# Layer 2's 512x512 product by seven block products, with its sums on GpSimd, and VectorE's set-up work moved

## The chip, the cores and the metric

One core of one Trainium2 chip runs the whole program. The metric is the device time of one execution in microseconds (us). All numbers are float32. The engines are called TensorE (PE; PEld is its weight load), VectorE (DVE), ScalarE (ACT), GpSimd (POOL) and SyncE (SP, which issues most DMAs).

## The reference, cut to what matters

Four residual layers act on x of 8 sequences of 128 tokens and width 512, 1024 tokens in all. Each layer has a first part (its conditioning) and a feed-forward part.

- Layer 0: a gated product with small per-sequence adapters, `silu(gate) * up` with 1376 hidden columns, a product back to 512, then a routed feed-forward.
- Layer 1: two chains of small adapters.
- Layer 2: attention with 32 query and 8 key heads of 128, over 512 cached positions (fetched through a block table) and the 128 new ones, then the feed-forward that this change is about.
- Layer 3: a routed product, then a second one with 64 small experts.

Layer 2's feed-forward, on the attention's output y:

```python
H = einsum('btd,od->bto', y, W) + b                     # the 512x512 product
z = einsum('btd,dr->btr', y, A)                         # rank 32
anchors = arange(1, T, 2)                               # every second token
H_slice = H[:, anchors, :8]
delta_slice = einsum('bar,er->bae', z[:, anchors], LiMEs)
H_scale = maximum(max(abs(H_slice)), EPS)               # one number over all tokens
d_scale = maximum(max(abs(delta_slice)), EPS)
probs = softmax(0.5 * H_slice / H_scale + 0.5 * delta_slice / d_scale)
...                                                     # weights: soft top 2 of 8, normalised
p_mix = einsum('bte,er->btr', repeat(weights, 2), LiMEs)
return H + einsum('btr,ro->bto', z * p_mix, Bmat) * 0.5
```

The result is added to x.

## The kernel before, in words

Activations lie feature by token: x is [128, 4, 1024], four chunks of 128 features. A product of 512 by 512 is done in blocks of 128, each f32 matmul of the program leaving two records in the trace.

**Two ways of multiplying.** The plain way uses eight products of half-size blocks. In most places the kernel uses seven instead (the scheme with sums s1 to s4 of the left blocks and t1 to t4 of the right ones, and three to four additions behind the products). `gates_by_seven` does so for layer 0's gates in stages f = 1 to 10, about 13.4 us each; the class `Seven` for layer 3. Its `begin` does the first product and copies it out, its `go_on` the others; the additions of its partial results (`u`, `p1`) are on VectorE, from PSUM banks `even` and `odd`. Layer 2's W was multiplied in the plain way by `product(b)`: one block of 128 tokens, 16 matmuls of 128 columns, eight times. The tile of its result is called h.

**Stages.** Loads and layer 0's gates of stage 0 (0 to 26 us; matmuls gu, rank sums tgm and tum); stages 1 to 10 of the gates (to 162; matmuls g, additions `up` and p); down product, layers 0 and 1 (to 297); attention in 32 steps (to about 1347); layer 2's feed-forward (to 1392); layer 3 (to the end).

**Attention's beginning.** Step n needs rows of the cache: `gather(n, "k")` and `gather(n, "v")` issue eight indirect DMAs each on GpSimd's queue. k's rows (tiles kn) are turned by a DMA (kt) ahead of the scores, v's rows (vals) are wanted by the step's last product, av. `run` orders them by hand: before the loop `gather(1, "v")` (L1326), in step 0 `gather(2, "k")` (L1379). The q products q_one, q_five, q_six are the seven-product scheme again.

**Layer 2's feed-forward.** At the end of the attention, `product(0)` already runs while the last step waits for R, the inverse sums that a DMA spreads over the partitions; then oT (av times R), its sums os, the out products wo_one to wo_six and their additions y. In `layer2`, `turn` transposes y into y2T for two last blocks of tokens, `low` gives z, `anchors` hd. `routing` reduces hd to big, GpSimd's partition_all_reduce gives top, and some twenty short instructions on VectorE and ScalarE (lg, p, m) give the weights. `gains` transposes them (pT), multiplies (pmix) and gives zp = z times p_mix. `delta(g)` adds zp by Bm to h with contraction 32, for half g of the tokens, and adds h to x. Between these, TensorE is filled with `product` and with the preparation of layer 3 (`weights_turned`: W3p, wB3p, copied by ScalarE to W; `fold_scores`: qwp, qbp, fkp, gkp). Layer 3 begins with midp, and then fp, the first `Seven`, whose left sums W3s are made by GpSimd (L2004), as are Bws. `anyone` is another partition_all_reduce on GpSimd, a check of the attention's sums, read at the end.

**Order.** Each engine runs its instructions in a fixed order. Where the code says `kept(...)`, an instruction stays behind the one traced before it on its engine; this sets the order of issue and is no wait. All else is placed by the framework's scheduler, by its own estimate of when inputs are ready; so the order on GpSimd and of the unpinned matmuls is not the order of the source. Matmuls of one PSUM bank and the VectorE instructions that read it wait for each other.

Of the kernel before, what the change touches and what calls it, by code (L numbers as in the profile page):

```python
# [47 lines left out]
def forward(ctx: ExitStack, tc: tile.TileContext, a: dict, out: bass.AP):  # L48
# [35 lines left out]
    for c in range(DC):  # L84
        sp.dma_start(x[:, c, 0:512], a["xT"][c * P : (c + 1) * P, 0:512])
        if c == 0:
            first = gate_weights(0, act, (slice(0, 1), slice(1, DC)))
            sp.dma_start(ids0_i, a["lora_ids"].partition_broadcast(P))
# [41 lines left out]
    def ints(name, n, where=const):  # L130
        ti = where.tile([P, n], I32, tag=name + "_i", name=name + "_i")
        sp.dma_start(ti, a[name].partition_broadcast(P))
        tf = where.tile([P, n], F32, tag=name, name=name)
        dve.tensor_copy(tf, ti)
        return tf

    def rows(name, n, where=const):
# [34 lines left out]
    mask1 = const.tile([P, NB], F32, tag="mask1", name="mask1")  # L172
    dve.tensor_scalar(mask1, ids1, p_div16, None, ALU.is_equal)

    kvrow = {}
    for what, order in (("v", "p (b c j) -> p b c j"), ("k", "p (b j c) -> p b c j")):
        selp = w0.tile([P, NB, 4, 4], F32, tag="selp", name="selp_" + what)
        dve.tensor_tensor(  # L180
            selp,
            table.rearrange(order, b=NB, c=4),
            block32.unsqueeze(1).unsqueeze(1).to_broadcast([P, NB, 4, 4]),
            ALU.mult,
        )
        page = const.tile([P, NB * 4], F32, tag="page", name="page_" + what)
        dve.tensor_reduce(page.rearrange("p (b c) -> p b c", c=4), selp, AX.X, ALU.add)
        dve.tensor_scalar(page, page, 32.0, p_mod32, ALU.mult, ALU.add)
        kvrow[what] = const.tile([P, NQ, NB * 4], I32, tag="kvrow_" + what, name="kvrow_" + what)
        for qd in range(NQ):  # L190
            dve.tensor_scalar(kvrow[what][:, qd, :], page, float(NQ), float(qd), ALU.mult, ALU.add)


    bias3 = const.tile([P, NB, 8], F32, tag="bias3", name="bias3")
    dve.tensor_tensor(
        bias3,
        eight.unsqueeze(1).to_broadcast([P, NB, 8]),
        lang.unsqueeze(2).to_broadcast([P, NB, 8]),
        ALU.is_equal,
    )  # L200
    dve.tensor_scalar(bias3, bias3, 5.0, None, ALU.mult)

# [115 lines left out]
    with c0:  # L318
# [75 lines left out]
        def gates(f, ws, between):  # L394

            fw = min(P, FF - f * P)
            banks = [bank(f"gu_{f}_{j}") for j in range(4)]
            for js in ((0, 1), (2, 3)):
                for c in range(DC):
                    if js[0] and c == 2:  # L400
                        between()
                    for k, w in enumerate(ws):
                        for j in js:
                            mmq(banks[j][:fw, k, :], w[:, c, :fw], x[:, c, quarter(j)], k == 0 and c == 0, False)
            return banks
# [25 lines left out]

        def gates_by_seven(f, A):

# [12 lines left out]
            for g in range(TG):  # L446
# [12 lines left out]
                kept(dve.tensor_tensor(p1, six[:, 0], p1, ALU.add))  # L459
                B.append((one, two, six, p1, u, b21, b22, t4))  # L460
            for one, two, six, _, _, b21, b22, t4 in B:
                into(one[:, 0], a12, b21, False)
                into(two[:, 1], s4, b22, False)
                into(six[:, 0], a22, t4, False)
# [74 lines left out]
        lora_gates(0, banks)  # L539
        rot, angles, turn_angles = rotary(tc, rp, w0, lens, part, rows, kept)  # L540
        for f in range(1, NF):
            after = f + 1 < NF and weight_sums(f + 1, gate_weights(f + 1))
            gates_by_seven(f, A)
            A = after
            if f == 2:
                down_loaded()
            for i in itertools.islice(angles, 3 * (f > 1)):
                kept(i)
            if f == NF // 2:
                AW = [down_weights(0, wop.tile([P, 3, NH, P], F32, tag="os", name="wds_0"))]  # L550
# [242 lines left out]
def attention(tc, a, x, ident, lens, kvrow, part, ww, wop, ypool, sums, rot, eps, psa, c2, chunks, mm):  # L793
# [524 lines left out]
    def run(pool_, end_of, bank, keep):  # L1318
# [6 lines left out]
        roots(1)  # L1325
        gather(1, "v")  # L1326
        rotated(1)
# [7 lines left out]
        for n, (qd, p) in enumerate(steps):  # L1335
# [41 lines left out]
            if n == 0:  # L1377
                next(sums_of)
                gather(2, "k")  # L1379
            every(sums_of)  # L1380
# [37 lines left out]
        every(outputs(n))  # L1418
        end.product(0, "st", bank)
        leave(n)  # L1420
# [312 lines left out]
def ending(  # L1733
# [57 lines left out]
    def load_w2():  # L1791
        W["2"] = tile_of_w2([P, DC, D], "WT2")
        kept(sp.dma_start(W["2"], chunks(a["W2T"])))
# [13 lines left out]
    def low(g, bank):  # L1807

        ps = bank("mm", [P, P], f"z2_{g}")
        for c in range(DC):  # L1810
            for j in range(HB):
                b = g * HB + j
                mmq(ps[slot(j), :], A2[:, c, :], Y2T[0][:, c, b * P : (b + 1) * P], c == 0, c == DC - 1)
        dve.tensor_copy(zq[:, g, :], ps)
# [10 lines left out]

    H = {}

    def shifted():

        for c in range(DC):  # L1830
            kept(act.activation(x[:, c, :], x[:, c, :], AF.Identity, bias=bcol[:, c : c + 1]))

    def product(b, tag, bank):

        ps = bank(tag, [P, DC, P], f"h_{b}")
        for o in range(DC):
            for c in range(DC):
                mmq(
                    ps[:, o, :], W["2"][:, c, o * P : (o + 1) * P], Y2T[0][:, c, b * P : (b + 1) * P],
                    o == 0 and c == 0, False,  # L1840
                )
        H[b] = ps

# [52 lines left out]
    def gains(bank):  # L1896
# [8 lines left out]
        for g in range(TG):  # L1905
            for j in range(HB):
                b = g * HB + j
                mmq(pm[slot(j), g, :], Li, pT[:, b * 64 : (b + 1) * 64], g == 0, True)
        zp = L3.w3.tile([P, TG, P], F32, tag="zp", name="zp")
        dve.scalar_tensor_tensor(  # L1910
            zp.rearrange("p g (t two) -> p g t two", two=2),
            zq.rearrange("p g (t two) -> p g t two", two=2),
# [3 lines left out]
            ALU.mult,  # L1916
        )
        Z["zp"] = zp

    def delta(g):  # L1920

        zp, Bm = Z["zp"], L3.Bm
        for o in range(DC):
            for j in range(HB):
                mmq(H[g * HB + j][:, o, :], Bm[slot(j), o * P : (o + 1) * P], zp[slot(j), g, :], False, True)
        for j in range(HB):
            b = g * HB + j
            t = x[:, :, b * P : (b + 1) * P]
            dve.tensor_tensor(t, H[b], t, ALU.add)

    def open3(w3, ex_sm):
# [21 lines left out]
        L3.steps = experts("l3", L3.wmr, "logits", 2.0, bias3, None, None, x, None, width=WR)  # L1955
        L3.zgT = w3.tile([P, DC, NT], F32, tag="zgT", name="zgT")

    def copied(shape, name, ps, dst=None):
# [18 lines left out]
    def fold_scores(bank):  # L1977
        ps = bank("mm", [P, D], "qwp")
        for o in range(DC):
            mmq(ps[slot(o), :], L3.wq[:, o, :], L3.W[:, o, :], True, True)  # L1980
        qw = copied([P, D], "qw3", ps)
        ps = bank("mm", [P, P], "qbp")
        for o in range(DC):
            mmq(ps[slot(o), :], L3.wq[:, o, :], L3.wBT[:, o, :], True, True)
        qb = copied([P, P], "qb3", ps)
# [20 lines left out]

    def right_sums(b11, b12, b21, b22, t):
        t1, t2, t3, t4 = (t[:, k] for k in range(4))
        for o, l, r in ((t1, b12, b11), (t2, b22, t1), (t3, b22, b12), (t4, b21, t2)):
            dve.tensor_tensor(o, l, r, ALU.subtract)  # L2010
        return b11, b21, b22, t1, t2, t3, t4
# [9 lines left out]
    class Seven:  # L2021
# [19 lines left out]
        def go_on(self):  # L2041
# [11 lines left out]
            self.into(even[:, 1], a22, t4)  # L2053

    S = {}

# [8 lines left out]
    def fold_ranks(bank):  # L2065
        L3.F = L3.w3.tile([P, DC, D], F32, tag="F3", name="F3")
        tw = room("o7", [P, 2, 4, 2, P], "W3s")
# [118 lines left out]

    def layer2(y2, bank, held=lambda: None, do=range(NB)):

        for b in do:
            turn(y2, b, bank)  # L2190
        for g in range(TG):
            if g or len(do) > HB:
                low(g, bank)
                anchors(g, bank)

        where = ["mm"]

        def free(tag, shape, name):
            return bank(where[0], shape, name)

        turning, folding = weights_turned(free), fold_scores(free)
        for b in range(HB):
            if b not in H:
                product(b, "av" if b == HB - 1 else "st", bank)
                next(turning, None)
        routing()
        gains(bank)
        product(HB, "av", bank)
        next(turning, None)
        delta(0)  # L2210
        where[0] = "st"
        for b in range(HB + 1, NB):
            product(b, "mm", bank)
            for _ in turning:
                pass
            next(folding, None)
        delta(1)

    def layer3(bank, between=lambda: None):
# [38 lines left out]
        prepare=prepare, load_w2=load_w2, load_aw=load_aw, turn=turn, low=low, anchors=anchors,  # L2258
        product=product, shifted=shifted, open3=open3, layer2=layer2, layer3=layer3,
    )  # L2260
# [65 lines left out]
```

## Time and profile before

| what | us |
|---|---|
| median of 3 runs (lowest, highest) | 1496.21 (1494.47, 1498.43) |
| profiled execution | 1493.37 |
| its span, first to last instruction | 1491.6 |
| TensorE busy (share of the span) | 1476.2 (99%) |
| VectorE, GpSimd, ScalarE busy | 1069.6, 855.0, 561.9 |
| windows of layer 2, 1343 to 1393: TensorE, VectorE, GpSimd busy | 49.4, 21.3, 10.4 of 50 |
| granted clock of TensorE | 1.00 |

A group line of the profile reads: line of the code, engine, operation, output<-input, shapes, count, then busy time and mean of one, and the idle time of its engine just ahead of it with what ended that. L followed by a number is a line of the kernel. A window line has the window, its length, then for PE, PEld, DVE, ACT and POOL the busy time with the number of instructions, the clock, the share of DMA and the GB/s. "Lost" time of TensorE, used below, is how much later a matmul started than the rate of its neighbours would have it; idle time, which the views print, is somewhat shorter, since a matmul's record runs past the start of the next.

### The profile page before, as it was taken

How to read it: one execution, taken by the hardware profiler on the slowest of the kernel's cores; microseconds unless marked ns; L12 is line 12 of the kernel's file. 1: busy time of each engine (PE TensorE's matmuls, PEld its weight loads, DVE VectorE, ACT ScalarE, POOL GpSimd, SP SyncE). 2: the span in 40 equal slices, each digit the busy share in tenths (PEclk: the TensorE clock that was granted, in tenths of full speed). 3: DMA queues.
4: the chain of work that ended last, by engine and by line, in shares of the span. 5: the costliest groups of instructions: out<-in, count | busy, mean ns of one | idle time of the engine just before them, and what ended most of it. 6: DMA issues, size and time to landing. Idle time of an engine off the chain costs nothing.

```text
span 1491.6 us, 18090 instructions
## 1 busy us (share of the span) xinstructions
PE 1476.2 (99%) x5603; PEld 937.3 (63%) x5603; DVE 1069.6 (72%) x2121; ACT 561.9 (38%) x1422; POOL 855.0 (57%) x876
## 2 busy tenths in 40 slices
PE   9999999999999999999999999999999999999998
PEld 7888787455555555555565555555555555559886
DVE  4665524388888787877778778777877878855475
ACT  1111101044444554444455445455445455431110
POOL 2242104567776777777677777677777767632310
PEclk9999999999999999999999999999999999999999
DMA  7411001213546444554444456445445534333001
GB/s 241 118 44 32 1 1 55 94 35 102 175 135 204 134 127 130 155 174 133 140 149 120 124 155 182 125 135 152 131 130 160 174 109 135 111 116 98 1 9 52
DMA packets 155082, 171.44 MB, mean 115 GB/s; under 512 B 52577, under 2 KB 125473, under 8 KB 154849
## 3 DMA queue, kind: packets, MB, share of 16 engines
q1 hardware_dynamic: 136832, 133.18, 30.4%
q0 software_dynamic: 17056, 36.49, 7.6%
q8 instruction: 47, 0.77, 0.2%
q10 hardware_dynamic: 1088, 0.52, 0.1%
q14 instruction: 59, 0.48, 0.1%
HBM read 129.36 MB, written 40.76 MB: 114 GB/s over the span
## 4 chain that ended last, share of the span: by engine, by line
PE 91%; DVE 3%; issue 2%; DMA 2%; ACT 0%; POOL 0%; SPq 0%; ACTq 0%; DVEq 0%; POOLq 0%
PE st L1165 18%; PE av L1217 17%; PE g L362 8%; PE q_six L971 8%; PE q_five L971 6%; PE q_one L971 5%; PE wo_two L971 5%; PE dn L362 5%; PE wo_six L971 4%; PE wo_one L971 4%; PE h L1753 2%; PE z L1753 2%; PE eo_l L53 2%; PE o L1753 1%; PE midp_l L53 1%
## 5 line engine op out<-in xcount | busy, mean ns | idle before, releaser
L914 POOL DMA_INDIRECT kn<-in_k_cache,kvrow_k x256 | 270.0, 1055 | 77.3 <-issue 71.8
L914 POOL DMA_INDIRECT vals<-in_v_cache,kvrow_v x256 | 271.6, 1061 | 73.5 <-issue 61.7
L1217 PE MATMUL av<-pT,vals 128*128 128x512 f32 x640 | 290.7, 592 | 0.2 <-DVE oT L1227 0.2
L1169 ACT ACTIVATE pT<-st,hide 128x512 f32<-128x512 f32 x256 | 175.9, 687 | 191.2 <-PE st L1165 167.9
L1165 PE MATMUL st<-qT,kT 128*128 128x512 f32 x512 | 236.0, 593 | 0.5 <-DMA qT<-turned_new 0.5
L1217 PEld LDWEIGHTS av<-pT,vals 128*128 128x128 f32 x640 | 121.4, 190 | 152.7 <-issue 149.5
L1070 POOL TENSOR_TENSOR vq<-q,txq 128x256 f32<-128x256 f32 x128 | 121.2, 976 | 135.7 <-ACT sqq L1044 95.5
L1165 PEld LDWEIGHTS st<-qT,kT 128*128 128x128 f32 x512 | 96.5, 190 | 109.5 <-issue 102.3
L1185 DVE TENSOR_TENSOR part<-pT 128x512 f32<-128x512 f32 x128 | 88.4, 691 | 76.6 <-ACT pT L1169 63.2
L971 PE MATMUL q_one<-q,x 128*128 128x384 f32 x256 | 93.0, 486 | 0.0
L1044 ACT ACTIVATE sqq<-q 128x128 f32<-128x128 f32 x252 | 78.2, 310 | 11.3 <-DVE q L1020 4.7
L971 PEld LDWEIGHTS q_one<-q,x 128*128 128x128 f32 x256 | 48.5, 190 | 39.8 <-issue 14.1
L971 PE MATMUL q_six<-q_s,xs_all 128*128 128x384 f32 x192 | 69.8, 486 | 0.0
L1025 ACT COPY q<-q_one 128x256 f32<-128x256 f32 x32 | 11.9, 372 | 152.1 <-PE q_one L971 133.5
L971 PE MATMUL wo_one<-o,oT 128*128 128x256 f32 x256 | 65.8, 379 | 0.3 <-DVE oT L1227 0.3
L1165 PE MATMUL st<-qT,kTn 128*128 128x512 f32 x128 | 65.4, 592 | 0.0
L971 PE MATMUL wo_two<-o_s,os 128*128 128x256 f32 x256 | 60.6, 380 | 0.3 <-DVE os L930 0.3
L1169 ACT ACTIVATE pT<-st,rs 128x512 f32<-128x512 f32 x64 | 44.0, 687 | 38.5 <-PE av L1217 16.5
L971 PEld LDWEIGHTS wo_one<-o,oT 128*128 128x128 f32 x256 | 48.6, 190 | 13.9 <-DVE oT L1227 0.5
L429 POOL TENSOR_TENSOR ws<-wu 128x256 f32<-128x256 f32 (+1 forms) x9 | 6.4, 712 | 88.4 <-DMA wu<-in_WuT 81.9
L1201 ACT COPY rows<-rows 32x32 f32<-32x32 f32 x96 | 20.7, 216 | 92.8 <-DVE rows L1196 85.9
L362 PE MATMUL g<-xs,ws 128*128 128x256 f32 (+1 forms) x240 | 55.1, 379 | 0.0
(461 smaller groups left out, 2843.5 us busy)
## 6 DMA issues: line engine op xcount, KB each, us to landing
turned_new<-qkt SPq DMA_DIRECT2D x120, 160.0 KB
turned_cached<-kt SPq DMA_DIRECT2D x128, 128.0 KB
kT<-turned_cached SPq DMA_DIRECT2D x32, 512.0 KB
R<-sums SPq DMA_DIRECT2D x32, 512.0 KB
qT<-turned_new SPq DMA_DIRECT2D x30, 512.0 KB
q<-in_WqT SPq DMA_DIRECT2D x8, 1024.0 KB
o<-in_WoT SPq DMA_DIRECT2D x8, 1024.0 KB
kn<-in_k_cache,kvrow_k POOLq DMA_INDIRECT x256
```

Source lines behind the costliest of these rows:

```text
L53: pe.matmul(o, lhsT, rhs, start=start, stop=stop)
L362: pe.matmul(o, lhsT, rhs, start=start, stop=stop, skip_group_check=True)
L914: kept(pool.indirect_dma_start(out=d[:, c, :], out_offset=None, in_=kc if what == "k" else vc, in_offset=bass.IndirectOffsetOnAxis(ap=kvro ...
L971: kept(pe.matmul(o, l[:, c, :], r[:, c, :], start=start and c == 0, stop=c == 1, skip_group_check=True))
L1044: kept(act.activation(sq, S[n][m][:, j, i, :], AF.Square, accum_out=S[n]["ssq"][:, j, col : col + 1]))
L1070: kept(pool.tensor_tensor(to, t[:, b, :, hi : hi + 64], wx[:, b, lo : lo + 64].unsqueeze(2).to_broadcast(list(to.shape)), ALU.mult,))
L1165: kept(pe.matmul(ps, s["kT"][:, c, 4 * j : 4 * j + 4, :] if c < 4 else s["kn"][:, j], s["qT"][:, :, REP * j : REP * (j + 1), :].rearrange( ...
L1169: kept(act.activation(pT[:, c, :, :].rearrange("p i t -> p (i t)"), ps, AF.Exp, **(dict(bias=hide[:, b, c : c + 1]) if c < 4 else dict(bia ...
L1185: kept(dve.tensor_tensor(o, l, r, ALU.add))
L1201: kept(act.copy(rows[0:32, g, :], rows[32 * g : 32 * g + 32, 0, :]))
L1217: kept(pe.matmul(ps, v[:, c, :], pT[:, c, :, :].rearrange("p i t -> p (i t)"), start=c == 0, stop=c == NC - 1, skip_group_check=True,))
L1753: return pe.matmul(o, lhsT, rhs, start=start, stop=stop, skip_group_check=True)
```

## The change

1. **Layer 2's product.** `product` is gone. `Second`, a subclass of `Seven`, does W times y2T in four parts (token half g, output half k), seven products each of 128x128 weights and 256 columns. Its opening (`second_begun`: products a11 b11, with the copy of it on ScalarE, and a12 b21) of the parts (0,0) and (0,1) takes the place of `product(0)` in the attention's last step. The sums of W and of both halves of y2T are made by GpSimd. Two of the four partial results go into x by separate additions of `u` and `p1`; the other half by `delta`, which adds now from four half banks per k.
2. **zp twice.** `gains` has zp a second time with neighbouring groups of 32 partitions exchanged, by four copies on ScalarE, since a bank of `Second` holds two blocks of tokens side by side.
3. **Order in layer 2.** `go_on` of (0,0) in front of `low` and `anchors`, (0,1) in front of `routing`; (1,0) is opened behind `routing` and continued behind `gains`; (1,1) behind `delta(0)`. `low` for g = 1, `delta`, qwp and qbp are pinned.
4. **VectorE's set-up.** The integer casts and the tables of the block table and of layer 3's bias (29 instructions) move from the start into stages f = 1 and 2 of the gates, ahead of `up`; the 23 angle instructions, three a stage, from behind a stage (f = 2 on) to ahead of `up` in it (f = 3 on).
5. **First loads.** The first chunk of x comes in two DMAs, the first gate weights in three pairs in place of two; the load of lora_ids goes behind x's second chunk; stage 0's first matmuls take the token halves one after the other.
6. **First gathers.** `gather(1, "v")` and `gather(2, "k")` exchange places.

The diff, cut to its core:

```diff
-            first = gate_weights(0, act, (slice(0, 1), slice(1, DC)))
+            first = gate_weights(0, act, (slice(0, 1), slice(1, 2), slice(2, DC)))
...
-        dve.tensor_copy(tf, ti)
+        to_float.append((tf, ti))
...
+    def tables():
+        for tf, ti in to_float:
+            yield dve.tensor_copy(tf, ti)
+        yield dve.tensor_scalar(mask1, ids1, p_div16, None, ALU.is_equal)
...
             B.append((one, two, six, p1, u, b21, b22, t4))
+            for i in meanwhile:
+                kept(i)
...
-            gates_by_seven(f, A)
+            gates_by_seven(f, A, itertools.islice(tabled, 15) if f < 3 else itertools.islice(angles, 3))
...
-            for i in itertools.islice(angles, 3 * (f > 1)):
-                kept(i)
...
-        gather(1, "v")
+        gather(2, "k")
...
-                gather(2, "k")
+                gather(1, "v")
...
-        end.product(0, "st", bank)
+        for k in range(2):
+            end.second_begun(0, k, bank("st", [P, 2, 256], f"h_0_{k}_even"))
...
-    def product(b, tag, bank):
-        ps = bank(tag, [P, DC, P], f"h_{b}")
-        for o in range(DC):
-            for c in range(DC):
-                mmq(
-                    ps[:, o, :], W["2"][:, c, o * P : (o + 1) * P], Y2T[0][:, c, b * P : (b + 1) * P],
...
+        for b in range(HB):
+            act.copy(zp[slot(b), 1], zp[slot(b ^ 1), 0])
...
-        for o in range(DC):
-            for j in range(HB):
-                mmq(H[g * HB + j][:, o, :], Bm[slot(j), o * P : (o + 1) * P], zp[slot(j), g, :], False, True)
-        for j in range(HB):
-            b = g * HB + j
-            t = x[:, :, b * P : (b + 1) * P]
-            dve.tensor_tensor(t, H[b], t, ALU.add)
+        for other in range(2):
+            for i in range(2):
+                for b in range(HB):
+                    k, h = b % 2, (b + other) % 2
+                    ps, o = H[g][k].c[i, b // 2][0], 2 * k + i
+                    kept(mmq(ps[:, h * P : (h + 1) * P], Bm[slot(b), o * P : (o + 1) * P], zp[slot(b), other, g, :], False, True))
+        for k, f in enumerate(H[g]):
+            for (i, j), (ps, _) in f.c.items():
+                t = x[:, 2 * k + i, g * 512 + j * 256 : g * 512 + (j + 1) * 256]
+                dve.tensor_tensor(t, ps, t, ALU.add)
...
+    class Second(Seven):
+        def __init__(self, even, g, k, p1, u):
+            self.A, self.B = left(W["2"], k), right(Y2T[0], g)
+            self.p1, self.u, self.even = p1, u, even
+            self.begin()
+            self.into(even[:, 0], self.A[1], self.B[2])
+        def go_on(self, odd, g, k):
...
+            self.into(odd[:, 1], s1, t1, True)
+            self.into(odd[:, 0], s2, t2)
+            dve.tensor_tensor(u, odd[:, 0], p1, ALU.add)
+            dve.tensor_tensor(p1, odd[:, 1], p1, ALU.add)
+            self.into(even[:, 1], s3, t3)
+            dve.tensor_tensor(p1, even[:, 1], p1, ALU.add)
+            yield
+            self.into(odd[:, 1], s4, b22)
+            self.into(even[:, 1], a22, t4)
+            self.c = {(0, 0): (even[:, 0], None), (0, 1): (odd[:, 1], u), (1, 0): (even[:, 1], u), (1, 1): (odd[:, 0], p1)}
+            for (i, j), (_, more) in self.c.items():
+                if more is not None:
+                    t = x[:, 2 * k + i, g * 512 + j * 256 : g * 512 + (j + 1) * 256]
+                    dve.tensor_tensor(t, t, more, ALU.add)
...
+        def sums():
+            t0 = [L3.w3.tile([P, 2, 256], F32, tag="zg", name=f"y2s_{i}", bufs=4) for i in range(4)]
+            Q["t", 0] = right_sums(*right(Y2T[0], 0), t0, pool)
+            tw = L3.F.rearrange("p c t -> p (c t)").rearrange("p (k a c n) -> p k a c n", k=2, a=4, c=2)
+            for k in range(2):
+                Q["w", k] = left_sums(*left(W["2"], k), tw[:, k], pool)
...
+        part = H[0][0].go_on(wide("st", 0, 0, "odd"), 0, 0)
+        next(part)
         for g in range(TG):
             if g or len(do) > HB:
                 low(g, bank)
                 anchors(g, bank)
...
-        for b in range(HB):
-            if b not in H:
-                product(b, "av" if b == HB - 1 else "st", bank)
-                next(turning, None)
+        every(part)
+        next(turning)
+        every(H[0][1].go_on(wide("av", 0, 1, "odd"), 0, 1))
+        next(turning)
         routing()
+        Q["t", 1] = right_sums(*right(Y2T[0], 1), t1, pool)
+        second_begun(1, 0, wide("av", 1, 0, "even"))
+        for _ in range(2):
+            next(turning)
         gains(bank)
-        product(HB, "av", bank)
-        next(turning, None)
+        every(H[1][0].go_on(wide("mm", 1, 0, "odd"), 1, 0))
         delta(0)
-        where[0] = "st"
-        for b in range(HB + 1, NB):
-            product(b, "mm", bank)
-            for _ in turning:
-                pass
-            next(folding, None)
+        for _ in turning:
+            pass
+        second_begun(1, 1, wide("st", 1, 1, "even"))
+        next(folding)
+        every(H[1][1].go_on(wide("st", 1, 1, "odd"), 1, 1))
+        for _ in folding:
+            pass
         delta(1)
```

## The prediction, made before the change was run

> **What bounds the kernel now.** I read the page first: TensorE is the bound, and the chain of waits agrees.
>
> ```profile
> span 1491.6 us, 18090 instructions
> PE 1476.2 (99%) x5603; PEld 937.3 (63%) x5603; DVE 1069.6 (72%) x2121; ACT 561.9 (38%) x1422; POOL 855.0 (57%) x876
> PE 91%; DVE 3%; issue 2%; DMA 2%; ACT 0%; POOL 0%; SPq 0%; ACTq 0%; DVEq 0%; POOLq 0%
> ```
>
> Only 15.4 us of the span are without a matmul. A part can gain in two ways: less TensorE work, or one of those gaps closed. So the second view is the windows by stage (PE, PEld, DVE, ACT, POOL busy; clock; DMA), for the stages touched:
>
> ```profile
> 26.00:162.00 136.00, 134.90 (x733) 111.70 (x726) 78.61 (x179) 21.30 (x61) 36.85 (x41) 1.00 0.22 61
> 350.00:358.00 8.00, 6.10 (x22) 4.04 (x23) 6.65 (x16) 4.01 (x20) 3.13 (x3) 1.00 0.31 83
> 1343.00:1360.00 17.00, 16.41 (x130) 14.18 (x128) 9.50 (x20) 3.02 (x5) 0.00 (x0) 1.00 0.69 213
> 1360.00:1393.00 33.00, 33.00 (x350) 31.20 (x351) 11.82 (x37) 4.89 (x12) 10.43 (x16) 1.00 0.01 1
> ```
>
> Layer 2 (last two rows) has a full TensorE whose weight loader is 31.2 of 33.0 us busy, and a GpSimd that does nothing to 1360. The waits by engine name the gaps (total, times, longest):
>
> ```profile
> PE q_six L971 <- DVE vals L1020: 1.4, 1, 1.4
> PE g L362 <- DVE p L457: 1.1, 2, 0.9
> PE q_five L971 <- issue: 0.9, 1, 0.9
> PE gu L362 <- DVE tgm L369: 0.3, 1, 0.3
> ```
>
> and where VectorE itself has room:
>
> ```profile
> DVE up L474 <- PE g L362: 48.0, 10, 5.6
> ```
>
> **What the Trainium skill says.** "TensorE: Matmul & The Clock Gate", section "LDWEIGHTS": a load's time goes with its columns (128 at 1.2 GHz, 107 ns). The trace agrees: the 128-column h records follow each other every 0.1143 us with the loader all but full. "GPSIMD Engine Reference", section 3.1: an add on GpSimd costs about twice VectorE's; here 128x512 takes 1.656 beside 0.685 us. Its section 2.1 has the first call of a freshly loaded library pay about 6 us; the trace has 6.0 before `anyone` (below) and, all-reduce to sum, 1362.5 to 1370.0. "SBUF — State Buffer", section "two separate sides": a VectorE instruction with two SBUF inputs and a GpSimd one exclude each other; L1075 goes from 1.26 to at most 1.78 us with GpSimd active.
>
> **Layer 2, TensorE.** From the timeline of TensorE (start, duration, count):
>
> ```profile
> 1343.28 3.74 PE L1753 MATMUL h<-y2T,WT 128*128 128x128 f32 x32
> 1347.35 1.13 PE L971 MATMUL wo_one<-o,oT 128*128 128x256 f32 x4 [0.34 <-DVE oT L1227]
> 1360.84 6.05 PE L1753 MATMUL h<-y2T,WT 128*128 128x128 f32 x52
> 1376.26 1.17 PE L1753 MATMUL h<-zp,Bm 32*128 32x128 f32 x32
> 1377.36 3.84 PE L1753 MATMUL h<-y2T,WT 128*128 128x128 f32 x32
> ```
>
> Removed: 256 records (an f32 matmul is two); 52 took 1360.84 to 1366.73, less a transition 0.1143 each: 29.3 us. Added: 4 (token half, output half) x 7 products x 2 x 2 = 112 records of 256 columns. wo_six and its neighbours of that width run 12 in 1351.62 to 1354.21: 0.2158 each, 24.2 us. That is 5.1 less. But 44 old records (5.0 us) lay in waits for the last attention step (32 of them for R before 1347.35, 12 more before 1355.6). Of the new ones the two openings, 16 records or 3.45 us, fit there, the rest depends on GpSimd's sums. On the path: 212 x 0.1143 = 24.2 against 96 x 0.2158 = 20.7: **3.5**; if `go_on` of (0,0) fills the late gaps, 4.4. I take 3.9. delta keeps 64 records of K=32. The pins of low, qwp and qbp, the longer W2 tile and F3's earlier place add no instruction: 0, with order their only effect, which is costed below where it makes something wait.
>
> **Layer 2, the others.** GpSimd gains 4 sums of 128x512 and 8 of 128x256 for the first half, 4 of 128x512 for the second:
>
> ```profile
> L2004 POOL TENSOR_TENSOR W3s<-W 128x256 f32<-128x256 f32 x4 | 2.8, 716 | 14.4 <-issue 14.4
> L1257 POOL TENSOR_TENSOR y<-y,uo 128x512 f32<-128x512 f32 x1 | 1.7, 1656 | 16.7 <-DVE y L1247 16.7
> L757 POOL PARTITION_ALL_REDUCE anyone<-some x1 | 0.4, 377 | 6.0 <-issue 6.0
> L1859 POOL PARTITION_ALL_REDUCE top<-big x1 | 0.4, 374 | 25.9 <-DVE big L1855 25.9
> ```
>
> 128x512 lies between 2 x 0.72 less a fixed part, 1.3, and 1.66. First half: 4 x 1.35 + 8 x 0.72 = 11.2 us, hidden in the 25.9 us before `top` (their tiles come to lie over pT of the last attention step, so they start when its last av ends, 1342.4, and end near 1354). The switch of 6.0 then ends at 1360, before `big` at 1361.7; that cover is 1.7 us. The second half's 5.4 us stand either ahead of `top` (their inputs are there at 1357, `big` at 1362) or behind it, with 7 us of switching, until about 1375.5 where product (1,0) wants them at 1373. Both have a price: ahead, `top` goes to about 1369, and ScalarE's W copies, for which the routing's `m` waits 3.2 us now, take up half of it. Bounds 0 and 3.7; I take **0.6**.
>
> VectorE: 8 additions of 128x512 (0.69) become 40 of 128x256 (0.42): 5.5 to 16.8 us. It is busy 11.8 of 33, so nothing by amount; but three stand in each product between matmuls that use the same bank. In layer 3 the same product loses 6.4 us to all waits over ten. 0 to 0.4 each, I take **0.5** for four. Product (1,1)'s bank comes free only after three additions behind delta(0), 1.2 us, of which wB3p covers 0.43: **0.7** (0 to 1.1), as the qwp and qbp behind it are pinned. GpSimd beside the oT and os that wo_one waits for: **0.3** (0 to 0.5). ScalarE's four copies of 32x256 (0.37 each, as q<-q_one) are needed 1.5 us behind zp, ready 1373.1 of the 1376.26 at which delta(0) goes: hidden with 1.7 us to spare. The x sums for `mids(0)` need delta(0) alone: nothing.
> Layer 2: 3.9 - 0.6 - 0.5 - 0.7 - 0.3 = **1.8** (-2 to 4.4).
>
> **Start.** The 23 angle instructions (r_sin up to 1.65 us) now run where `up` waits, 4.8 us per stage, three of about 1.1 = 3.4 us. That takes away the two waits of g, in lost time 1.05 (88.55) and 0.38 (115.72): **1.4** (1.0 to 1.4). The tables (29 short ones, 2.6 and 2.0 us) leave VectorE's queue ahead of tgm: gu's wait at 25.11, 0.28 idle and 0.44 lost, goes: **0.4** (0 to 0.5); without them tgm could go near 23.1. Splitting x and the first weights adds two DMA issues, on SP and ACT, some 0.5 us; gu follows the warm-up matmuls without a gap, so 0; with its cover gone 0.5. The lora_ids behind them have 4 us before AgT at 16.3.
>
> **Gathers.** Eight DMA issues of some 1.26 us each swap places on GpSimd's queue: k's rows of step 2 come 10 us earlier (now landing 352.1, kt turns them at 353.3), v's of step 1 as much later, about 352.5, where av wants them at 363.7. TensorE lost 1.01 (350.52) and 1.54 (353.46). But VectorE's late start at 349.9 has no rows behind it: its product had ended at 347.1. At most 2.5, at least 0; I take **1.0**. No loss, with 11 us of margin.
>
> **Sum.** 1.8 + 1.4 + 0.4 + 1.0 = 4.6 us off the profiled 1493.37 (span 1491.6 and 1.8 around it): 1488.8. That execution lies 2.8 below the median of 1496.21, so **1491.6**. A measurement can tell about 0.3%, 4.5 us, from no change: the forecast stands just at that bound.
>
> **Rivals.**
> 1. GpSimd's queue becomes the bound. Sums at 1.66 and 0.98 beside VectorE end at 1357.1, the second half's at 1363.8, the switch at 1369.8: `top` 7.7 us late. Layer 3's W3s sums stand behind it on the same queue, two more switches away: those that the first product needs end at 1392.6 and its first fp of them goes at 1398.7, a margin of 6.1. A slip of 7.7 puts that fp 1.6 later than before, whatever TensorE saved ahead of it, and all after it: **1497.8**, slower. It decides from a `top` 6.1 us late, and delta(0), with a margin of 1.7, waits first. For it: one queue in order, and switches of 6 to 7 us in the trace; against: a W3s sum may be put ahead of `anyone`, and ScalarE's slack. 0.16.
> 2. The gap at 350 is no matter of the gathers, and the products lose 0.4 each, the bank 1.1: 4.6 - 1.0 - 1.1 - 0.4 = 2.1, **1494.1**. 0.21.
> 3. All closes: gathers 2.5, layer 2 3.5, start 1.8: 7.8, **1488.4**. For it: layer 2 holds filler matmuls for every wait. 0.21.
>
> **Numbers.** Forecast 0.42 (1490 to 1493), rivals 0.16, 0.21, 0.21. Below 1491.7: rival 3 and nearly three quarters of the forecast, 0.51; above 1500.7: the worse third of rival 1 (a switch more), 0.06; between: 0.43. Range 1487 to 1498: from under rival 3 to just short of rival 1.
>
> **What would show it.** Right: no idle at 25.1, 88.6 and 115.7; `up`'s wait for g some 35 us shorter; h in 112 records of 256 columns near 0.216; midp after layer 2 four to six us earlier than 1392.3. Wrong: `top` later than 1364, zp later than 1375, idle of TensorE before delta(0) or fp with a GpSimd releaser; the gap at 350 still there.

## The result and the profile after

The changed kernel takes 1510.82 us (median; 1508.56 to 1511.03) beside 1495.34 for the kernel before on the same chip: ratio 1.0094, 95% interval 1.0075 to 1.0113. By the ratio it is 14 us **slower** (15.5 between the two medians), where 4.6 us faster was forecast. The profiled execution took 1510.69 us.

The page of the changed kernel shows a TensorE that is busy 2.3 us more, on a span 17.3 us longer, with 144 fewer records (5459 for 5603), as forecast:

```profile
span 1508.9 us, 17880 instructions
PE 1478.5 (98%) x5459; PEld 933.3 (62%) x5459; DVE 1076.0 (71%) x2153; ACT 565.3 (37%) x1430; POOL 871.5 (58%) x892
```

The windows of the changed kernel (columns as before: PE, PEld, DVE, ACT, POOL, granted clock, DMA, GB/s), with the last one added because layer 2 now ends at 1407 and not at 1392:

```profile
26.00:162.00 136.00, 136.00 (x744) 113.11 (x737) 80.11 (x210) 22.40 (x64) 37.36 (x42) 1.00 0.23 65
350.00:358.00 8.00, 6.97 (x29) 5.51 (x30) 7.15 (x15) 6.35 (x26) 4.75 (x6) 1.00 0.39 104
1343.00:1360.00 17.00, 14.68 (x72) 11.71 (x71) 10.71 (x18) 4.57 (x8) 11.64 (x12) 1.00 0.69 212
1360.00:1393.00 33.00, 27.82 (x212) 21.52 (x211) 20.05 (x59) 6.86 (x16) 17.98 (x22) 0.95 0.01 1
1393.00:1408.00 15.00, 8.46 (x58) 7.20 (x57) 5.00 (x15) 0.58 (x2) 0.38 (x1) 0.73 0.00 0
```

The gates (first row) have no idle time left. Layer 2 has 14.0 us of it (65 less 50.96) where before had 0.6, and in its second half the clock column falls to 0.95 and 0.73. A full engine has become one with eleven groups of waits; the main ones of this stretch (total, times, longest):

```profile
PE h_odd L1762 <- DVE p_h L2080: 4.1, 2, 3.5
PE midp_l L53 <- DVE x L1937: 3.0, 1, 3.0
PE pT L1904 <- DVE p L1896: 1.4, 1, 1.4
PE y2T L1815 <- DVE y L1265: 1.0, 1, 1.0
PE h_even L1762 <- DVE x L1937: 0.9, 1, 0.9
PE wo_two L979 <- DVE os L938: 0.9, 1, 0.9
PE pmix L1762 <- ACT pTs L1906: 0.7, 1, 0.7
```

To compare kernels, I take from each trace the time from the last av (end of the attention) to the first fp, which stands behind layer 3's first product midp: 55.9 us before, **71.2** in the changed kernel. I call it layer 2's time. It is 15.3 of the 17.3 us. 3.4 more lie in the attention, where the waits for qT's DMA are 3.0 us in place of 0.5, and 1.0 behind the first fp; 2.4 were gained up to 355 us.

**What holds the largest wait.** The chain that ended last, in order of time (start, duration, what), shortly before the end of layer 2:

```profile
1391.11 5.51 issue
1396.62 0.39 POOL anyone L765
1397.01 0.02 issue
1397.03 0.04 DVE redo_i L766
1397.06 0.04 issue
1397.11 0.43 DVE u_h L2079
...
1397.57 0.43 DVE p_h L2080
...
1398.05 2.08 PE h_odd L1762 x4
```

`redo_i` is the integer cast of `anyone`, the check of the attention's sums, which no instruction of layer 2 reads. The scheduler put it on VectorE's queue ahead of product (1,1)'s additions. `anyone` came at 1396.6 (before: 1383.2). Most of this is that GpSimd's queue was late as a whole: its first sum behind `top` started at 1379.3, and at 1370.0 before. The rest, about 4 us, is that six more W3s sums than before stood ahead of `anyone`. The switch to the all-reduce is no longer than it was (5.75 us, 6.05 before). In VectorE's timeline:

```profile
1397.03 0.15 DVE L766 CAST redo_i<-anyone 128x1 int32<-128x1 f32 x1 [7.01 <-POOL anyone L765]
1397.11 0.42 DVE L2079 TENSOR_TENSOR u_h<-h_odd,p_h 128x256 f32<-128x256 f32 x1
```

In the kernel before, the same cast waited too, but the next instruction on VectorE's queue came only 8.7 us later:

```profile
1383.61 0.15 DVE L758 CAST redo_i<-anyone 128x1 int32<-128x1 f32 x1 [3.67 <-POOL anyone L757]
1392.43 2.48 DVE L1929 TENSOR_TENSOR x<-h,x 128x512 f32<-128x512 f32 x4 [8.67 <-PE h L1753]
```

The last matmul of the chain shows the second cost: its four records take about 1.9 us, 0.47 each on the mean and 0.43 behind the first, in place of 0.216. Three windows on the slow records, of the changed kernel:

```profile
1379.60:1383.00 3.40, 3.40 (x12) 2.72 (x9) 0.42 (x1) 1.61 (x4) 3.40 (x6) 0.52 0.00 0
1398.00:1403.00 5.00, 4.96 (x18) 4.12 (x18) 1.32 (x4) 0.37 (x1) 0.00 (x0) 0.50 0.00 0
1407.30:1410.30 3.00, 3.00 (x10) 3.00 (x10) 0.00 (x0) 0.00 (x0) 0.00 (x0) 0.53 0.02 5
```

Each stretch follows idle time, and TensorE is busy in it at half clock: 3.4 x 0.48 + 5.0 x 0.50 + 3.0 x 0.47 = 5.5 us lost. The Trainium skill, "TensorE: Matmul & The Clock Gate", section "What's actually happening", says that the clock is gated to half after an idle window of about 3.4 us. The half is what we see, but no window ahead of these three was wholly idle; the last section works out what they have in common.

The sum for layer 2: 13.4 us more idle time and 5.5 of clock, less what the new product saves. By the count of records that is 5.1. In e4 and e12 below, whose clock was full in layer 2, its time without the idle time is 51.5 and 51.6 us for 55.3 before, so it is 3.7 to 3.8; with 3.7 the sum is 15.2 of the 15.3.

### The profile page after: what moved, and what is told of

Its sections match the earlier page's. It is cut to its first block, busy times and chain, and to the rows that moved or that the text cites. A ratio compares the mean times of both kernels' runs of the same rounds, so it can differ in the third digit from the quotient of the medians.

```text
span 1508.9 us, 17880 instructions
## 1 busy us (share of the span) xinstructions
PE 1478.5 (98%) x5459; PEld 933.3 (62%) x5459; DVE 1076.0 (71%) x2153; ACT 565.3 (37%) x1430; POOL 871.5 (58%) x892
```

## The experiments

The ratio of each is to the kernel before, run beside it on the same chip, with its 95% interval. "Layer 2" is layer 2's time in its one trace, and "idle" the idle time of TensorE in it, which is counted apart from its clock. The median of the kernel before was 1494.51 beside e1 to e4, 1494.12 beside e5 to e8, 1495.13 beside e9 to e11 and 1492.14 beside e12; so runs of different groups are compared by their ratios.

| run | median us | ratio (interval) | layer 2, us | idle, us |
|---|---|---|---|---|
| before | 1495.34 | | 55.9 | 0.6 |
| changed kernel | 1510.82 | 1.0094 (1.0075 to 1.0113) | 71.2 | 14.0 |
| e1, e11: start's parts alone | 1494.26, 1493.07 | 0.9993 (0.9978 to 1.0007), 0.9986 (0.9975 to 0.9997) | 56.4, 56.4 | 1.0, 1.1 |
| e2: layer 2 alone | 1513.46 | 1.0115 (1.0086 to 1.0144) | 72.3 | 15.0 |
| e3: gathers back | 1513.40 | 1.0119 (1.0090 to 1.0148) | 74.1 | 14.8 |
| e4: redo_i on GpSimd | 1500.72 | 1.0042 (1.0030 to 1.0054) | 62.7 | 11.2 |
| e5: e4 + bank | 1495.70 | 1.0013 (1.0000 to 1.0025) | 60.5 | 7.0 |
| e6: e4 + second sums on VectorE | 1499.56 | 1.0043 (1.0032 to 1.0055) | 65.7 | 10.1 |
| e7: e4 + layer 3's sums later | 1499.42 | 1.0038 (1.0028 to 1.0048) | 65.1 | 10.7 |
| e8: e4 + these three | 1496.61 | 1.0019 (1.0008 to 1.0031) | 62.0 | 7.4 |
| e9: e8 + routing first | 1495.76 | 0.9999 (0.9988 to 1.0009) | 61.2 | 5.9 |
| e10: e9 + fold ahead | 1496.04 | 0.9998 (0.9985 to 1.0011) | 59.0 | 5.1 |
| e12: e10 + ScalarE's order | 1487.81 | 0.9972 (0.9964 to 0.9981) | 54.4 | 2.8 |

The theory after the first look: the loss is all in layer 2, and it is made by the order of single instructions on VectorE, GpSimd and ScalarE and by banks, not by the amount of work on any of them. The rivals: the moved gathers, or the seven products as such.

**e1, start's parts alone**: the hunks of parts 4 to 6 of the diff above, on the kernel before; nothing of layer 2.

> The kernel before with parts 4 to 6 alone (first loads, tables and angles, first gathers); layer 2 by the old product. In the changed kernel's trace these stages stand 1.6 us ahead of before at 297 us and 2.4 to 2.7 ahead at 355 to 505; by 1291 us 4.0 have been lost again, in four or five waits of the scores for qT<-turned_new. Theory (layer 2 is the whole loss, the qT waits are chance): 2 to 2.7 us faster than before, about 1493. Rival (the moved gathers or tables bring the qT waits): about 1497, slower than before by 1 to 2.

0.9993: not told apart from the kernel before by its interval, whose upper end, 1.0007, is 1495.6 and so excludes the rival's 1497. e11 repeated it.

**e2, layer 2 alone**: the hunks of parts 1 to 3, on the kernel before; tables, angles and gathers stay where they were.

> The kernel before with parts 1 to 3 alone (seven products, zp twice, order in layer 2). Theory: layer 2 is the whole loss, some 15.3 us between the last av and the first fp: about 1510.5, and fp starts 15 us later than before's 1397.9. Rival (part of it is the throttled clock or a state that the moved gathers bring): under 1506.

1513.46, layer 2 at 72.3 us: all the loss is there without any of the other parts. (In its trace `h_odd` waits 4.9 us at the cast.)

**e3, gathers back**

```diff
-        gather(2, "k")
+        gather(1, "v")
...
-                gather(1, "v")
+                gather(2, "k")
```

> The changed kernel with gather(1,v) and gather(2,k) in their old places. Theory (the gathers gained 0.8 us at 350 and nothing else): 0.5 to 1 us slower than the changed kernel, about 1511.5. Rival (they bring the qT waits of the attention, 3 to 4 us): 3 us faster, about 1508.

1513.40: no gain, so the rival falls; the qT waits are also in this trace (three, 2.3 us). Over all traces the attention from the first out product to the last av takes 985.5 to 990.6 us with the new order of the gathers and 987.1 to 992.4 with the old. I take the qT waits as chance of DMA landings; that is not shown, as no run was made on them.

**e4, redo_i on GpSimd**

```diff
-        dve.tensor_copy(redo_i, anyone)
+        pool.tensor_copy(redo_i, anyone)
```

> The changed kernel with one instruction moved: redo_i, the integer cast of anyone, on GpSimd in place of VectorE. Theory (in the trace it stands in VectorE's queue ahead of the additions of the last product, waits 7.0 us for anyone, which GpSimd gives only after its switch at 1396.6, and TensorE idles 3.5 us there and then runs at about half clock): the wait of h_odd for p_h goes, 3.5 us plus some 2 to 3 of clock, about 1505. Rival (the end of layer 2 is set by the routing chain and by banks anyway, the cast only fills a gap): 1510, within 1 us of the changed kernel.

More than expected: layer 2 falls by 8.5 us, the ratio from 1.0094 (1.0115 and 1.0119 for e2 and e3) to 1.0042. 3.5 us of this are the wait and 3.9 the half clock in the two windows that lie behind it (2.5 and 1.4 us of the 5.5). The first window, at 1379.6, lies ahead of the wait and can't come from the cast; e4's execution has 1.00 there too. By ratio e4 gains 7.8 us on the changed kernel, about the 7.4 of wait and clock, and 10.9 and 11.5 on e2 and e3, whose traces have longer waits there (4.9 and 4.1 us). These differences are uncertain by some 3 to 4 us; what e2 and e3 lose beyond that was not settled. One cast of 128x1 was worth 55% of the loss by the changed kernel's ratio, 64% by those of e2 and e3. TensorE's waits that are left in e4:

```profile
PE midp_l L53 <- DVE x L1937: 3.0, 1, 3.0
PE pT L1904 <- DVE p L1896: 1.4, 1, 1.4
PE wo_two L979 <- DVE os L938: 1.4, 1, 1.4
PE y2T L1815 <- DVE y L1265: 1.0, 1, 1.0
```

**e5, the bank**

```diff
-        every(H[1][1].go_on(wide("st", 1, 1, "odd"), 1, 1))
+        every(H[1][1].go_on(wide("mm", 1, 1, "odd"), 1, 1))
```

> The kernel of redo on GpSimd, with one PSUM tag changed: the odd bank of product (1,1) from st to mm. Theory (midp, layer 3's first product, was given the bank of that product and idles 3.0 us there until the last of delta(1)'s eight additions; now its bank is one that was free long before): midp starts right behind delta(1), 2.5 to 3.2 us are gained, 1497.5 to 1498.2. Rival (midp needs the x that these additions make, or W3s and the routing of layer 3 keep fp where it is): 1500.7, the wait stays or moves to fp.

The first line of the list above is gone from e5's waits, the ratio falls to 1.0013; by ratio 4.3 us, in layer 2's time 2.2, though in e5's trace the clock takes back 1.7. midp now starts right behind delta(1)'s last matmul, ahead of the eight additions. So it had not waited for x, as the view names it, but for a PSUM bank: the allocator had given it the one that these additions free last.

**e6, the second half's sums on VectorE**

```diff
-        Q["t", 1] = right_sums(*right(Y2T[0], 1), t1, pool)
+        Q["t", 1] = right_sums(*right(Y2T[0], 1), t1)
```

> The kernel of redo on GpSimd, with the sums t of the second half of y2T (zgT) by VectorE in place of GpSimd. Theory (these sums stand in GpSimd's queue ahead of its 6 us switch and of top, and put the routing 8.5 us late against big at 1361.7): the switch ends near 1358 to 1361, top comes with big; PE's waits for p and pTs (1.6 and 0.8 lost) go and VectorE's additions beside GpSimd get shorter; top at 1366 or earlier against 1370.2, 2 to 3 us gained, about 1498.5. Rival (VectorE's queue, which holds 5.3 us of layer 3's sums ahead of hd, sets big and so top anyway, and now has 2.8 us more): top at 1369 to 1370, nothing gained, 1500 to 1501.

A miss for both. `top` was made at 1358.5, so GpSimd was out of the way; but nothing was gained by ratio, and TensorE's wait for p grew from 1.4 to 2.9 us. VectorE took `top` up only at 1363.4.

**e7, layer 3's sums later**

```diff
-        S["a"] = right_sums(*right(W["a"], 0), ts[:, 0])
+        b11, b12, b21, b22 = right(W["a"], 0)
+        t1, t2, t3, t4 = (ts[:, 0, k] for k in range(4))
+        for o, l, r in ((t1, b12, b11), (t2, b22, t1), (t3, b22, b12), (t4, b21, t2)):
+            kept(dve.tensor_tensor(o, l, r, ALU.subtract))
+        S["a"] = b11, b21, b22, t1, t2, t3, t4
```

> The kernel of redo on GpSimd, with layer 3's four sums of AwT on VectorE pinned behind delta(1)'s additions, so that they no longer stand ahead of the additions of product (0,0) and of hd. Theory (GpSimd's switch sets top): PE's 1.0 us before h_odd at 1362.9 and some slowness by shared SBUF access go, top stays at 1370 since GpSimd's queue holds it; 0.5 to 1 us gained, 1500; unless fp now waits for the sums (2.7 us behind 1397, fp at 1403: no). Rival (VectorE's queue sets the routing): top 4 us earlier, 3 us gained, 1497.5.

As expected in kind: big came 2.9 us sooner (1362.5 for e4's 1365.4), but `top` hardly moved (1369.3 for 1370.2), since GpSimd's queue held it. By ratio 0.6 us, within the interval of e4.

**e8, the three together**: the hunks of e5, e6 and e7 on e4.

> The kernel of redo on GpSimd with the three edits together (bank, second half's sums on VectorE, layer 3's sums later). Theory: both queues ahead of top are freed, big near 1363, top with it, midp without wait: 3.0 + 2.4 + 1 to 2 gained, 1493.5 to 1495, as the kernel before or up to 1 us faster. Rival (the pieces cover one another, or the bank's qwp copy and delta's additions now set the pace): 1497.

Not better than the bank alone, in ratio, layer 2's time or idle time: the rival. The reason is in VectorE's timeline of e8:

```profile
1358.40 0.27 DVE L1858 TENSOR_REDUCE big<-hd 128x1 f32<-128x32 f32 x2
1361.95 0.42 DVE L2079 TENSOR_TENSOR WT<-h_odd,WT 128x256 f32<-128x256 f32 x1 [3.28 <-PE h_odd L1762]
...
1363.41 0.75 DVE L2090 TENSOR_TENSOR x<-x,WT 128x256 f32<-128x256 f32 x2
1364.08 0.16 DVE L1864 TENSOR_SCALAR top<-top 128x2 f32<-128x2 f32 x1
```

and in GpSimd's:

```profile
1358.81 0.38 POOL L1862 PARTITION_ALL_REDUCE top<-big  x1 [9.66 <-DVE big L1858]
```

`top` is there at 1359.2; VectorE stands idle for 3.3 us at product (0,1)'s first addition, which waits for TensorE, and begins the routing 4.9 us late.

**e9, routing first**

```diff
-        every(H[0][1].go_on(wide("av", 0, 1, "odd"), 0, 1))
-        next(turning)
         routing()
+        every(H[0][1].go_on(wide("av", 0, 1, "odd"), 0, 1, kept))
+        next(turning)
```

(`go_on` passes the last argument to its first addition.)

> The kernel of the three edits together, with routing traced ahead of go_on(0,1) and that product's first addition on VectorE pinned behind it. Theory (with GpSimd out of the way top was ready at 1359.2, but VectorE took it only at 1364.1, behind six additions of product (0,1) that wait for TensorE; so VectorE's order holds the routing now): the routing runs 4.5 to 5 us earlier, TensorE's wait for p (3.1 lost) and most of that for pTs go, and as filler (1,0)'s opening and W3p stand ahead of pT: 3 to 3.5 us gained on the kernel of the three edits, 1493 to 1493.6, ratio to before about 0.9995. Rival (the additions of (0,1), late now, hold its bank and TensorE waits there or at delta(0) instead): 1495 to 1497.

The routing's first instruction now follows `top` by 0.04 us. p is ready 9.3 us after GpSimd has made `top`, in place of 12.5 in e8, and the ratio improved by 0.0020, or 3.0 us: what was expected in size, though the two intervals touch and layer 2 is only 0.8 us shorter in its one trace. The routing itself became slower: from its first instruction on VectorE to p it takes 9.2 us, in place of 7.6 in e8. A third queue held it.

**e10, fold ahead**

```diff
-        second_begun(1, 1, wide("st", 1, 1, "even"))
         next(folding)
+        second_begun(1, 1, wide("st", 1, 1, "even"))
```

> As routing first, and besides qwp and qbp ahead of the opening of product (1,1). Theory (that opening waits 0.9 us for the bank that delta(0)'s additions free, and qwp and qbp, 1.1 us of matmuls, were pinned behind it): the wait of h_even for x goes; 0.9 us on top of the run with routing first, 1492 to 1492.7. Rival (they need W3's last copy or delay p_h's copy and its successors by the same amount): no difference.

The wait of 0.9 us is gone from its trace; the times can't tell it from e9. ScalarE's timeline of e10 shows the queue in question, p being the routing's first exponential, whose input was there about 1361.7:

```profile
1362.18 0.59 ACT L1969 COPY W<-W3p 128x512 f32<-128x512 f32 x1 [8.13 <-PE W3p L1978]
1364.35 0.59 ACT L1969 COPY W<-W3p 128x512 f32<-128x512 f32 x1 [1.58 <-PE W3p L1978]
1365.22 0.37 ACT L2048 COPY p_h<-h_even 128x256 f32<-128x256 f32 x1 [0.28 <-PE h_even L1762]
1365.48 0.23 ACT L1877 ACTIVATE p<-lg 128x32 f32<-128x32 f32 x1
```

Two copies that wait for TensorE stand ahead of an instruction that was ready.

**e11, start again**: the kernel of e1, without an edit.

> The kernel before with parts 4 to 6 alone, once more, beside the two above. Theory (the angles and tables gain the 1.6 us that the gates' stages show in every trace, 26 to 161 us; the rest of the start and the gathers is chance): 1.0 to 2.0 us faster than before, ratio 0.9988 to 0.9993. Rival (the earlier 0.9993 was noise): 1.0000.

0.9986 (0.9975 to 0.9997): parts 4 to 6 gain about 2 us (0.4 to 3.7).

**e12, ScalarE's order**

```diff
-            copied(None, None, ps.rearrange("p c d -> p (c d)"), L3.W[:, o, :])
+            i = act.copy(L3.W[:, o, :], ps.rearrange("p c d -> p (c d)"))
+            if o:
+                kept(i)
...
-            self.begin()
+            self.into(even[:, 0], self.A[0], self.B[0], True)
+            kept(act.copy(p1, even[:, 0]))
```

> As fold ahead, and besides ScalarE's copies of W3p (all but the first) and of the openings pinned behind the routing's m. Theory (with VectorE's order mended the routing starts at 1360.3 with top, but its first exponential ran only at 1365.5, behind a W copy and the copy of (1,0)'s opening, both waiting for TensorE; ScalarE's order is the third queue that holds it): p ready 2.5 us earlier, the 2.2 us lost before pT go, and with them most of the lowered clock between 1360 and 1393 (0.95 granted, 1.6 us); 2 to 3.5 us gained on fold ahead, 1492.5 to 1494, at or under the run with the start's parts alone. Rival (TensorE has no filler ahead of pT any more, as (1,0)'s opening waits for its copy behind m): the same idle time one place earlier, 1495.5 to 1496.5.

1487.81, ratio 0.9972 (0.9964 to 0.9981): 4.2 us **faster than the kernel before**, and the fastest of all; by ratio 3.9 us better than e10, somewhat more than expected. From the routing's first instruction to p it now takes 5.8 us, and TensorE has no hole between 1360 and 1380. Its ScalarE timeline, p and m ahead of the copies:

```profile
1361.42 0.23 ACT L1877 ACTIVATE p<-lg 128x32 f32<-128x32 f32 x1
1362.98 0.23 ACT L1888 ACTIVATE m<-m 128x32 f32<-128x32 f32 x1 [1.32 <-DVE m L1887]
1363.11 0.57 ACT L1979 COPY W<-W3p 128x512 f32<-128x512 f32 x1
```

and two rows of its windows, with the clock at 1.00:

```profile
1360.00:1370.00 10.00, 10.00 (x72) 8.44 (x71) 7.96 (x27) 3.45 (x8) 4.06 (x6) 1.00 0.00 1
1370.00:1380.00 10.00, 10.00 (x81) 7.04 (x80) 6.80 (x17) 3.32 (x8) 8.15 (x11) 1.00 0.01 2
```

So the seven products do save time in layer 2 (54.4 us against the old 55.9 to 56.4), once a bank, four orders and the engine of two steps are set. About 2 of the 4.2 us are those of parts 4 to 6 (e11). Of these edits e4 and e5 were shown one by one; the share of each of the others was not measured in the finished kernel. What the same edits would give the old product was not run; with 0.6 us of idle time in its layer 2, it has little to win from them there.

## Why the prediction was wrong

**Right.** The product's 112 records of 256 columns at 0.216 us. As for what it saves, TensorE's busy time in layer 2 at full clock is 3.7 to 3.8 us less, where the records were to give 5.1; the other 1.3 were not broken down. The gates: the stages from the first g to the last took 134.8 us before (136.6 in e2, of which 1.7 by half clock) and 133.2 in every kernel with the moved angles, 1.6 for the forecast 1.4. The bank of product (1,1): 0.9 us for 0.7. The POOL branch: the second half's sums did go ahead of `top`, with 5.7 us of switching. The 2.8 forecast for parts 4 to 6 (1.8 for tables and angles, 1.0 for the gathers) lie within the intervals of e11 and e1, which have 2.1 and 1.0. That e12 ends near the forecast 4.6 is no success of the prediction: it has seven edits that the predicted kernel lacks.

**The step that failed first** is the sentence on VectorE, "It is busy 11.8 of 33, so nothing by amount". Amount was the wrong measure. I asked which additions stand between matmuls of a bank, not what else could stand ahead of them in VectorE's queue. `redo_i` was in the trace before, with its wait of 3.7 us for `anyone` and nothing due behind it; the change put additions behind it that TensorE needs. Rival 1 even had all of GpSimd's queue slipping by 7.7 us with `top` (it was 9.7), but I followed it only to W3s and fp. That place did not fail: the scheduler put the W3s sums ahead of `anyone`, and fp waited for none of them. By e4 this omission is worth more than half of the loss. How long the cast waited follows from the third step below; that VectorE and TensorE waited with it follows from this one.

**The second** is "The x sums for `mids(0)` need delta(0) alone: nothing". True of the data; the wait was on the bank (3.0 us, e5), and I did not ask which bank midp would be given.

**The third** is the routing term, 0.6 with bounds 0 to 3.7. `top` came at 1371.8, past the 1364 that was to count as wrong: the sums by GpSimd beside VectorE took up to 1.72 us each, with a W sum between them, and its queue started them at 1358.8, where their inputs had been put at 1357. TensorE lost 1.4 and 0.7 us there, and 1.6 of clock behind them. But GpSimd was not the whole of it: e6 freed it and gained nothing, and the traces of e8 and e10 show VectorE's order and then ScalarE's behind it. "ScalarE's slack" was no slack but a queue, in order, with copies that wait for TensorE.

**The fourth** was absent: idle time of TensorE was priced at its own length. With 3.4 to 6.8 us at half clock behind it, some of it costs nearly twice (14.0 us of idle time brought 5.5 of clock). The estimate of the layer's range, -2 at worst, had no such term.

Small terms: GpSimd beside os cost 0.6 (0.9 less the 0.3 of before; forecast 0.3 with oT); y2T's 1.0 was not forecast, it was covered before by ten records of the old product. `up`'s wait became 9 us shorter (48.0 before), not 35. I take it that this is because the angles stood in the same stages before: VectorE's busy time from 26 to 162 us rose by 1.5 us only, from 78.6 to 80.1.

```profile
DVE up L483 <- PE g L367: 38.9, 10, 5.4
```

One reading of the prediction proves less than it says: L1075 takes 1.26 us in 23 of its 32 instances and 1.77 to 1.78 in 9, but GpSimd is active through the short ones too, so the two lengths don't tell GpSimd's presence from its absence.

The tables' 0.4 did not show: g starts at 26.4 us for 26.2 before, and at 25.4 to 28.0 in the other traces, as the first loads land.

**Rival 2**'s word on the gap at 350 is undecided: a gap of over 1 us stands in all three traces with the old order of the gathers, and still in three of the eleven with the new one, the changed kernel's among them (1.7 us). So the new order did not close it for certain; whether it makes it rarer, and what makes it, stays open. Rival 1 named GpSimd's queue as the cause on the slow side, which is a part of what happened; its victim was another.

## What to carry to other kernels

When work is added to a stage, list for each engine's queue what is in front of the new instructions and what that waits for, above all the instructions that had idle time before them and nothing behind them until now: their wait is free only while nobody stands there. Expect a lifted queue to show the next: here the routing was held by GpSimd, then VectorE, then ScalarE; freeing the first gave nothing by itself (e6), the second 3.0 us by ratio (e9) and the third 3.9 (e12). And price a hole of a few microseconds in a full TensorE at more than its length, because of the clock.

## What the runs showed of the hardware

**The clock.** In the fourteen traces every change of the granted clock during the work lies a whole number of 3.41 us from the others of its trace, and the half-clock stretches are one or two such lengths. If a trace is cut along this grid, the windows explain themselves. The changed kernel, with TensorE's busy time as the first number behind the length and the clock as the third from the end:

```profile
1376.02:1379.43 3.41, 1.31 (x23) 0.60 (x21) 1.74 (x9) 0.81 (x2) 0.10 (x1) 1.00 0.01 2
1379.43:1382.84 3.41, 3.41 (x23) 2.64 (x13) 0.42 (x1) 1.61 (x4) 3.41 (x6) 0.50 0.00 0
1393.09:1396.50 3.41, 1.44 (x9) 1.17 (x7) 0.00 (x0) 0.00 (x0) 0.00 (x0) 1.00 0.00 0
1396.50:1399.91 3.41, 1.86 (x4) 1.51 (x5) 2.26 (x7) 0.00 (x0) 0.38 (x1) 0.50 0.00 0
```

The holes ahead of pT and pmix, 1.43 and 0.66 us with four transpose records between them, fall into one window here, which is busy for 1.31 of 3.41 us; the next one runs at half clock. In e4 the first of the same two holes lies across a border of the grid, both windows are busy for 2.3 us, and the clock stays, as it does around the 3.0 us ahead of midp (windows busy for 1.95 and 1.86 us):

```profile
1372.46:1375.87 3.41, 2.32 (x11) 1.72 (x11) 2.91 (x18) 1.35 (x4) 0.00 (x0) 1.00 0.02 5
1375.87:1379.28 3.41, 2.29 (x26) 1.76 (x27) 0.73 (x3) 1.30 (x3) 1.59 (x3) 1.00 0.00 0
1379.28:1382.70 3.42, 2.88 (x16) 2.08 (x14) 2.69 (x6) 1.47 (x4) 3.42 (x5) 1.00 0.00 0
```

Over all traces, without the last 25 us of each: of the windows at full clock, all 12 in which TensorE was busy for under 45% are followed by one at half clock, 6 of 12 between 45 and 55%, and 4 of nearly 6000 above that, for which I have no explanation. So a window need not be idle, as the Trainium skill's page has it; here half empty was enough. The grid lies differently in each trace, so the same waits cost differently in two executions. Layer 2's time in e6 and e7 (65.7 and 65.1 us) contains 10.2 and 6.8 us at half clock, and is not to be read against e4's 62.7, which has none; the idle times can be.

**GpSimd.** In e4 it ran the cast of `anyone` 0.06 us behind the all-reduce (1395.07 and 0.38 long, cast at 1395.51). In the kernel before, 7.45 and 6.92 us stood between an all-reduce and the next addition on it, for which the profile names no releaser.
